# Four graph layers on one core: self loops on the adjacency's diagonal, the GCN weight behind its aggregation, two norms from one variance, and a lag of six steps

## The chip, the cores and the metric

The kernel runs on one core of a Trainium2 chip. The metric is the device time of one execution in microseconds; all times here are microseconds unless marked otherwise. The core's engines are TensorE (PE in the profile; PEld is its weight load), VectorE (DVE), ScalarE (ACT), GpSimd (POOL) and SyncE (SP). Each takes its own instructions in a fixed order, and they wait for each other by semaphores.

## What is computed

32 graphs of 512 tokens with 256 features, each with its own dense 512x512 adjacency, pass through four layers. Everything is float32. `_layernorm` has no scale or shift; `ln` is a layer norm with gamma and beta.

```
# layer 0, GIN
agg = adj @ x;   h = (1 + eps) * x + agg
x = _layernorm(x + relu(h @ W1 + b1) @ W2 + b2)          # hidden size 512
# layer 1, GCN
h = adj @ (x @ W.T + b)
x = _layernorm(x + where(h > 0, h, alpha * h))
# layer 2, GraphConv on the normalised input
h = ln(x, gamma, beta)
x = _layernorm(x + (x + relu((adj @ h) @ W_rel + b_rel + h @ W_root)))
# layer 3, GIN with RMS norm and SiLU
agg = eps * x + adj @ x
h = silu(rmsnorm(agg @ W1 + b1) * w)                     # hidden size 1024
x = _layernorm(x + h @ W2 + b2)
```

## The kernel before

The adjacency is laid out on the host so that a graph's tile `adjT` [128, 4, 512] holds, for each chunk `m` of 128 source tokens, all 512 target tokens. A token-major tile is [128, 4, 256] (four chunks of 128 tokens), a feature-major one [128, 2, 512]. PSUM has four buffers, each of two banks, for all products (`mm_feat`, `mm_tok`).

A graph is a Python generator, `graph`, that yields after each step. It has 15 steps. Layer 0 adds b2 to x on GpSimd (`xb`, L198), transposes x (L119), scales the transpose by 1+eps on ScalarE (L201), aggregates (`aggregate_feat`, L129) and sums the two on VectorE (L204); then come the hidden layer (`dense_feat`, L156, with ReLU on ScalarE, L212), the output product (`dense_tok`, L144), the residual (L216) and the norm. A norm is `row_stats` and `layernorm`: statistics for four chunks (L169, L171), variance plus epsilon (L173), the power -1/2 on GpSimd (L175), and four scaled chunks (L182). Layer 1 transposes x, multiplies by W, adds b (L227), aggregates token-major (L232), and forms the leaky ReLU with one ScalarE and two VectorE passes (L240 to L244). Layer 2 takes statistics again of the normalised x, applies gamma and beta in eight VectorE ops (L253, L256), doubles x on GpSimd (L260), transposes h, aggregates it, and multiplies both by their weights in one sum (L269). Layer 3 is like layer 0, with eight hidden chunks; each is evicted by VectorE (L295), squared by ScalarE (L300) and added up by GpSimd (L301). Products with a column of ones (L307) give the sum over features, four transposes (L319) spread 1/rms, and L323 and L324 scale and apply SiLU.

Two generators (`stream`) handle the even and the odd graphs; a loop advances them in turns, the second one step behind (`LAG = 1`). Loads of a graph are asked for two graphs ahead into three buffers. The framework's scheduler sets the order of instructions on each engine at build time, in program order as far as dependencies and free buffers allow it, and puts in the semaphores. So the loop's order matters, but the built order decides.

Of the kernel before, what the change touches and what calls it, by code (L numbers as in the profile page):

```python
# [18 lines left out]
def tile_gnn_stack(ctx: ExitStack, tc: tile.TileContext, a: dict, out: bass.AP):  # L19
    """Four adjacency layers, each with a residual and a layer norm, one graph at a time.  # L20

    Token t of a graph sits on partition t // NC in chunk t % NC, in every tile.
    Token-major tiles are [P, NC, D]; feature-major ones [P, D // P, N] with
    their columns ordered (chunk, partition).
    """
# [24 lines left out]
    def row(name):  # L50
        """A feature vector on every partition."""
        v = a[name]
        t = const.tile([P, v.shape[0]], F32, tag=name, name=name)
        nc.gpsimd.dma_start(t, v.partition_broadcast(P))
        return t

    def col(name):
        """A feature vector down the partitions, one column for each chunk of P."""
        v = a[name]
        t = const.tile([P, v.shape[0] // P], F32, tag=name, name=name)  # L60
        with nc.allow_non_contiguous_dma(reason="a small vector, once"):
            nc.gpsimd.dma_start(t, v.rearrange("(c p) -> p c", p=P))
        return t
# [11 lines left out]
    mhalf = const.tile([P, NC], F32, tag="mhalf", name="mhalf")  # L75
# [4 lines left out]
    eps3 = row("L3_gnn_epsilon")  # L80
    one_eps0 = const.tile([P, 1], F32, tag="one_eps0", name="one_eps0")
    nc.vector.tensor_scalar(one_eps0, eps0, 1.0, None, op0=ALU.add)
    nalpha = const.tile([P, 1], F32, tag="nalpha", name="nalpha")
    nc.vector.tensor_scalar(nalpha, alpha, -1.0, None, op0=ALU.mult)

    b1_0 = col("L0_gnn_b1")
    b2_0 = row("L0_gnn_b2")
    b_1 = row("L1_gnn_b")
    b_2 = row("L2_gnn_b_rel")
    g_2 = row("L2_gnn_ln_gamma")  # L90
    be_2 = row("L2_gnn_ln_beta")
    b1_3 = col("L3_gnn_b1")
    w_3 = col("L3_gnn_rms_weight")
    b2_3 = row("L3_gnn_b2")

# [7 lines left out]

    def over_tokens(t):
        return t.unsqueeze(1).to_broadcast([P, NC, D])

# [7 lines left out]
    def transposed(x):  # L114
        """Token-major x to feature-major, in PSUM."""
        ps = mm_feat()
        for j in range(DC):
            for c in range(NC):
                nc.tensor.transpose(  # L119
                    ps[:, j, c * P : (c + 1) * P], x[:, c, j * P : (j + 1) * P], ident  # L120
                )
        return ps

    def aggregate_feat(x, adjT):
        """(adj @ x) transposed, feature-major, in PSUM."""
        ps = mm_feat()
        for j in range(DC):
            for m in range(NC):
                nc.tensor.matmul(  # L129
                    ps[:, j, :],  # L130
                    x[:, m, j * P : (j + 1) * P],
                    adjT[:, m, :],
                    start=(m == 0),
                    stop=(m == NC - 1),
                )
        return ps

    def dense_tok(pairs):
        """sum of xT.T @ W over the pairs, token-major, in PSUM."""
        ps = mm_tok()  # L140
        steps = [(xT, W, k) for xT, W in pairs for k in range(W.shape[1])]
        for c in range(NC):
            for i, (xT, W, k) in enumerate(steps):
                nc.tensor.matmul(  # L144
                    ps[:, c, :],
                    xT[:, k, c * P : (c + 1) * P],
                    W[:, k, :],
                    start=(i == 0),
                    stop=(i == len(steps) - 1),
                )  # L150
        return ps

    def dense_feat(ps, i, xT, W, f):
        """Chunk f of (x @ W) transposed into slot i of a feature-major PSUM tile."""
        for k in range(DC):
            nc.tensor.matmul(  # L156
                ps[:, i, :],
                W[:, k, f * P : (f + 1) * P],
                xT[:, k, :],
                start=(k == 0),  # L160
                stop=(k == DC - 1),
            )

    def row_stats(r):
        """Mean and 1 / sqrt(variance + eps) of each token: [P, NC, 2] and [P, NC]."""
# [6 lines left out]
        ve = small.tile([P, NC], F32, tag="ve", name="ve")  # L172
        nc.vector.tensor_scalar(ve, mv[:, :, 1], LN_EPS, None, op0=ALU.add)  # L173
        rstd = small.tile([P, NC], F32, tag="rstd", name="rstd")
        nc.gpsimd.tensor_tensor(rstd, ve, mhalf, op=ALU.pow)  # L175
        return mv, rstd

    def layernorm(r, name):
        mv, rstd = row_stats(r)
        y = work.tile([P, NC, D], F32, tag=name, name=name)  # L180
        for c in range(NC):
            nc.vector.tensor_scalar(  # L182
                y[:, c, :], r[:, c, :], mv[:, c, 0:1], rstd[:, c : c + 1],
                op0=ALU.subtract, op1=ALU.mult,
            )
        return y

    def tok(name):
        return work.tile([P, NC, D], F32, tag=name, name=name)

    def feat(name):
        return work.tile([P, DC, N], F32, tag=name, name=name)

# [1 line left out]
    def graph(b, x, adjT):  # L195
        # layer 0: GIN
        xb = tok("xb")
        nc.gpsimd.tensor_add(xb, x, over_tokens(b2_0))  # L198
        pT = transposed(x)
        xT = feat("xT")  # L200
        nc.scalar.activation(xT, pT, AF.Identity, scale=one_eps0)  # L201
        pa = aggregate_feat(x, adjT)
        aT = feat("aT")
        nc.vector.tensor_add(aT, pa, xT)  # L204
        yield
        h1 = work.tile([P, FC0, N], F32, tag="h1", name="h1", bufs=1)
# [9 lines left out]
        nc.vector.tensor_add(r, ps, xb)  # L216
        x = layernorm(r, "x1")
        yield

        # layer 1: GCN  # L220
        pT = transposed(x)
        xT = feat("xT")
        nc.scalar.activation(xT, pT, AF.Copy)
        yield
        ps = dense_tok([(xT, W_1)])
        h = tok("h")
        nc.vector.tensor_add(h, ps, over_tokens(b_1))  # L227
        yield
        ps = mm_tok()
        for c in range(NC):  # L230
            for m in range(NC):
                nc.tensor.matmul(  # L232
                    ps[:, c, :],
                    adjT[:, m, c * P : (c + 1) * P],
                    h[:, m, :],
                    start=(m == 0),
                    stop=(m == NC - 1),
                )
        neg = work.tile([P, NC, D], F32, tag="neg", name="neg", bufs=1)
        nc.scalar.activation(neg, ps, AF.Relu, scale=-1.0)  # L240
        s = tok("s")
        nc.vector.scalar_tensor_tensor(s, neg, nalpha, x, op0=ALU.mult, op1=ALU.add)
        r = tok("r")
        nc.vector.scalar_tensor_tensor(r, ps, 0.0, s, op0=ALU.max, op1=ALU.add)  # L244
        x = layernorm(r, "x2")
        yield

        # layer 2: GraphConv on the normalised input
        mv, rstd = row_stats(x)
        t = tok("s")  # L250
        h = tok("h")
        for c in range(NC):
            nc.vector.scalar_tensor_tensor(  # L253
                t[:, c, :], x[:, c, :], mv[:, c, 0:1], g_2, op0=ALU.subtract, op1=ALU.mult
            )
            nc.vector.scalar_tensor_tensor(  # L256
                h[:, c, :], t[:, c, :], rstd[:, c : c + 1], be_2, op0=ALU.mult, op1=ALU.add
            )
        xx = tok("xb")
        nc.gpsimd.tensor_add(xx, x, x)  # L260
        yield
        pT = transposed(h)
        hT = feat("xT")
        nc.scalar.activation(hT, pT, AF.Copy)
        pa = aggregate_feat(h, adjT)
        aT = feat("aT")
        nc.scalar.activation(aT, pa, AF.Copy)
# [3 lines left out]
        nc.vector.tensor_add(t, ps, over_tokens(b_2))  # L271
        r = tok("r")
        nc.vector.scalar_tensor_tensor(r, t, 0.0, xx, op0=ALU.max, op1=ALU.add)
# [3 lines left out]
        # layer 3: GIN with RMS norm and SiLU  # L277
        xb = tok("xb")
        nc.gpsimd.tensor_add(xb, x, over_tokens(b2_3))
        pT = transposed(x)  # L280
        xT = feat("xT")
        nc.scalar.activation(xT, pT, AF.Identity, scale=eps3)
        pa = aggregate_feat(x, adjT)
        aT = feat("aT")
        nc.vector.tensor_add(aT, pa, xT)
# [19 lines left out]
        pq = psum.tile([P, DC, N], F32, tag="ps", name="pq")  # L305
# [8 lines left out]
        rstd = small.tile([P, NC], F32, tag="rstd", name="rstd")  # L314
        nc.gpsimd.tensor_tensor(rstd, ve, mhalf, op=ALU.pow)
        yield
        pr = psum.tile([P, DC, N], F32, tag="ps", name="pr")
# [10 lines left out]
        nc.vector.tensor_add(r, ps, xb)  # L328
# [5 lines left out]
    LAG = 1  # L334
    AHEAD = 2
    loaded = {b: load_graph(b) for b in range(min(AHEAD, B))}

# [54 lines left out]
```

## Time and profile before

| what | us |
|---|---|
| median of 3 runs (3096.54 to 3097.55) | 3096.62 |
| span of the profiled execution | 3094.4 |
| mean granted TensorE clock | 0.964 of full speed |
| L156, hidden layers: PE busy, idle before | 726.0, 51.8 |
| L144, all dense products: PE busy | 1086.9 |
| L129, feature-major aggregations: PE busy | 685.7 |
| L232, token-major aggregation: PE busy, idle before | 252.1, 28.9 |
| L119, transposes of x and of h: PE busy, idle before | 169.3, 72.4 |
| L307, sums of squares: PE busy, idle before | 43.5, 58.1 |
| L198, L260, L279, three GpSimd passes over a token tile | 75.3, 60.5, 75.4 |
| L301, GpSimd sums of squares | 284.1 (1.268 each) |
| adjacency load of a graph, issue to landing | 4.8 |

Busy time is what an engine spends inside instructions, idle is the time just before such an instruction in which the engine had nothing to do. A line number is that of the kernel above. A matmul of float32 appears as two instructions. "x8 [1.33 <-DVE x L182]" means eight instructions, before which the engine stood idle for 1.33, until VectorE finished writing x at line 182.

### The profile page before, as it was taken

To read this page: it belongs to the slowest core of one execution; us is meant where nothing else is said; L and a number is where in the kernel's file an instruction comes from. 1 tells how busy PE (TensorE), PEld (TensorE's weight loads), DVE (VectorE), ACT (ScalarE), POOL (GpSimd) and SP (SyncE) were. 2 spreads that over 40 slices of the span, in tenths; PEclk is the share of its full clock that TensorE was granted. 3 is DMA by queue.
4 is the path that set the end of the run, shared out by engine and by line. 5 is a ranking of instruction groups with operands and counts; after the bars stand their busy time and mean duration, and the time that the engine had idled before them with its cause. 6 is when DMAs were issued, how large, how long until landed. Compare 5 with 4: busy or idle time off the path is not lost.

```text
span 3094.4 us, 25923 instructions
## 1 busy us (share of the span) xinstructions
PE 2861.3 (92%) x10112; PEld 1838.1 (59%) x10112; DVE 1275.2 (41%) x3044; ACT 617.7 (20%) x834; POOL 699.3 (23%) x530
## 2 busy tenths in 40 slices
PE   8999899998999989999899999999999899998997
PEld 4556565665656656566565665647656466564654
DVE  1535335343353443434435253442534435343353
ACT  1131221212112121221212212121121211212112
POOL 1221312213031131311313113131131312313122
PEclk9999999999999999999999999999999999999998
DMA  3000000000000000000000000000000000000000
GB/s 136 28 21 8 27 28 27 28 1 27 28 28 28 8 28 21 28 28 14 28 14 27 28 14 28 14 27 28 14 28 14 28 28 14 28 7 14 14 1 14
DMA packets 17355, 73.49 MB, mean 24 GB/s; under 512 B 1937, under 2 KB 4241, under 8 KB 13137
## 3 DMA queue, kind: packets, MB, share of 16 engines
q1 hardware_dynamic: 13824, 67.12, 6.2%
q10 hardware_dynamic: 2928, 3.93, 0.4%
q8 instruction: 79, 1.29, 0.2%
q0 software_dynamic: 480, 0.80, 0.1%
q14 instruction: 44, 0.35, 0.0%
HBM read 55.06 MB, written 16.78 MB: 23 GB/s over the span
## 4 chain that ended last, share of the span: by engine, by line
PE 77%; DVE 14%; POOL 4%; ACT 3%; issue 2%; DMA 1%; POOLq 0%; ACTq 0%; DVEq 0%
PE pst L144 29%; PE psf L129 21%; PE psf L156 18%; PE pst L232 4%; PE psf L119 3%; DVE st L169 3%; DVE hT L295 2%; POOL rstd L175 2%; DVE x L182 2%; PE pq L307 1%; ACT sq L300 1%; POOL acc L301 1%; DVE h L227 1%; DVE hT L323 1%; DVE h L256 1%
## 5 line engine op out<-in xcount | busy, mean ns | idle before, releaser
L156 PE MATMUL psf<-aT,L_gnn_W 128*128 128x512 f32 x1536 | 726.0, 615 | 51.8 <-ACT sq L300 36.5
L156 PEld LDWEIGHTS psf<-aT,L_gnn_W 128*128 128x128 f32 x1536 | 283.2, 192 | 406.5 <-issue 268.0
L175 POOL TENSOR_TENSOR rstd<-ve,mhalf 128x4 f32<-128x4 f32 x160 | 165.2, 1033 | 1464.2 <-DVE ve L173 1448.1
L144 PE MATMUL pst<-L_gnn_W,hT 128*128 128x256 f32 x2048 | 480.4, 398 | 4.8 <-ACT hT L324 4.8
L129 PE MATMUL psf<-adjT,x 128*128 128x512 f32 x1024 | 458.0, 595 | 3.7 <-DMA adjT<-in_adj_dram 3.7
L144 PEld LDWEIGHTS pst<-L_gnn_W,hT 128*128 128x128 f32 x2048 | 410.3, 201 | 73.2 <-issue 7.2
L301 POOL TENSOR_TENSOR acc<-acc,sq 128x512 f32<-128x512 f32 x224 | 284.1, 1268 | 283.2 <-ACT sq L300 278.2
L129 PEld LDWEIGHTS psf<-adjT,x 128*128 128x128 f32 x1024 | 189.7, 192 | 217.0 <-issue 212.9
L295 DVE TENSOR_SCALAR hT<-psf,L_gnn_b 128x512 f32<-128x512 f32 x256 | 191.5, 748 | 251.1 <-PE psf L156 235.7
L232 PE MATMUL pst<-h,adjT 128*128 128x256 f32 x1024 | 252.1, 408 | 28.9 <-DVE h L227 28.9
L232 PEld LDWEIGHTS pst<-h,adjT 128*128 128x128 f32 x1024 | 208.3, 206 | 70.2 <-DVE h L227 39.2
L182 DVE TENSOR_SCALAR x<-r,mv,rstd 128x256 f32<-128x256 f32 x512 | 176.9, 409 | 141.7 <-POOL rstd L175 141.7
L129 PE MATMUL psf<-adjT,h 128*128 128x512 f32 x512 | 227.7, 592 | 0.0
L144 PE MATMUL pst<-L_gnn_W,h 128*128 128x256 f32 x1024 | 226.3, 379 | 0.0
L300 ACT ACTIVATE sq<-psf,L_gnn_b 128x512 f32<-128x512 f32 x224 | 146.9, 685 | 392.1 <-DVE hT L295 388.5
L328 DVE TENSOR_TENSOR r<-pst,xb 128x1024 f32<-128x1024 f32 x32 | 39.2, 1225 | 431.0 <-PE pst L144 431.0
L144 PEld LDWEIGHTS pst<-L_gnn_W,h 128*128 128x128 f32 x1024 | 193.3, 190 | 37.1 <-issue 12.3
L212 ACT ACTIVATE h<-psf,L_gnn_b 128x512 f32<-128x512 f32 x128 | 88.0, 687 | 567.5 <-PE psf L156 567.5
L198 POOL TENSOR_TENSOR xb<-x,L_gnn_b 128x1024 f32<-128x1024 f32 x32 | 75.3, 2354 | 508.4 <-DVE r L328 508.4
L324 ACT ACTIVATE hT<-hT,L_gnn_rms_weight 128x512 f32<-128x512 f32 x256 | 166.1, 713 | 78.8 <-DVE hT L323 78.7
L169 DVE BATCH_NORM_STATS2 st<-r 128x6 f32<-128x256 f32 x512 | 179.4, 413 | 2.7
L119 PE MATMUL psf<-ident,x 128*128 128x128 f32 x768 | 125.2, 282 | 48.8 <-DVE x L182 43.9
(60 smaller groups left out, 2195.4 us busy)
## 6 DMA issues: line engine op xcount, KB each, us to landing
adjT<-in_adj_dram SPq DMA_DIRECT2D x32, 1024.0 KB, 4.8
x<-in_x_dram SPq DMA_DIRECT2D x32, 512.0 KB, 3.6
out_dram<-x SPq DMA_DIRECT2D x32, 512.0 KB, 2.6
L_gnn_W<-in_L_gnn_W_dram ACTq DMA_DIRECT2D x2, 1024.0 KB, 15.7
L_gnn_W<-in_L_gnn_W_dram ACTq DMA_DIRECT2D x2, 512.0 KB, 12.2
L_gnn_b<-in_L_gnn_b_dram POOLq DMA_DIRECT2D x3, 128.0 KB, 8.0
L_gnn_W<-in_L_gnn_W_dram ACTq DMA_DIRECT2D x1, 256.0 KB, 19.9
L_gnn_W_rel<-in_L_gnn_W_rel_dram ACTq DMA_DIRECT2D x1, 256.0 KB, 20.0
```

The lines of the kernel that those rows point to most:

```text
L119: nc.tensor.transpose(ps[:, j, c * P : (c + 1) * P], x[:, c, j * P : (j + 1) * P], ident)
L129: nc.tensor.matmul(ps[:, j, :], x[:, m, j * P : (j + 1) * P], adjT[:, m, :], start=(m == 0), stop=(m == NC - 1),)
L144: nc.tensor.matmul(ps[:, c, :], xT[:, k, c * P : (c + 1) * P], W[:, k, :], start=(i == 0), stop=(i == len(steps) - 1),)
L156: nc.tensor.matmul(ps[:, i, :], W[:, k, f * P : (f + 1) * P], xT[:, k, :], start=(k == 0), stop=(k == DC - 1),)
L169: nc.vector.bn_stats(st[:, c, :], r[:, c, :])
L175: nc.gpsimd.tensor_tensor(rstd, ve, mhalf, op=ALU.pow)
L182: nc.vector.tensor_scalar(y[:, c, :], r[:, c, :], mv[:, c, 0:1], rstd[:, c : c + 1], op0=ALU.subtract, op1=ALU.mult,)
L232: nc.tensor.matmul(ps[:, c, :], adjT[:, m, c * P : (c + 1) * P], h[:, m, :], start=(m == 0), stop=(m == NC - 1),)
L295: nc.vector.tensor_scalar(hT[:, f, :], ps[:, i, :], bias, None, op0=ALU.add)
L300: nc.scalar.activation(sq, ps[:, i, :], AF.Square, bias=bias)
L301: nc.gpsimd.tensor_add(acc, acc, sq)
L324: nc.scalar.activation(hT[:, f, :], hT[:, f, :], AF.Silu, scale=w_3[:, f : f + 1])
```

## The change

Self loops: GpSimd copies the four 128x128 diagonal blocks of `adjT` into `dg` and adds a scaled identity onto the diagonal in place (`loop0`, (1+eps) times identity). So the aggregation of layer 0 gives the sum with (1+eps)x itself, and the transposes and the sum are gone. After it, the diagonal is put back from `dg`; after layer 2's aggregation, `loop3` (eps times identity) is put on it for layer 3.

GCN: `adj @ (x @ W.T + b)` becomes `(adj @ x) @ W.T + rowsum(adj) * b`. The row sums come from three GpSimd additions (`rows`) and four products with ones (`rs`).

Two norms: the input of layer 2 is the norm of a norm. Its scale follows from the first variance, so one set of statistics and one power op of eight columns give both the normalised h and the doubled x. Gamma is folded into the layer 2 weights and beta into two rows (`shift_rel`, `shift_2`) once at the start; `u` applies them with the row sums.

`aggregate` moves each half of its result out of PSUM by ScalarE as soon as that half is complete. Residual sums run in halves of the tile. `transposed` goes by chunk first. A graph has 14 steps, and the second stream starts six steps behind (`LAG = 6`). The tiles `dg`, `rows`, `u` and `v` are new; `h1` has two buffers.

```diff
+    def diagonal(adjT):
+        flat = adjT.rearrange("p m n -> p (m n)")
+        step = N + P
+        return [flat[:, m * step : m * step + P] for m in range(NC)]
...
-    mhalf = const.tile([P, NC], F32, tag="mhalf", name="mhalf")
+    mhalf = const.tile([P, 2 * NC], F32, tag="mhalf", name="mhalf")
...
+    loop0 = const.tile([P, P], F32, tag="loop0", name="loop0")
+    nc.vector.tensor_scalar(loop0, ident, one_eps0, None, op0=ALU.mult)
+    loop3 = const.tile([P, P], F32, tag="loop3", name="loop3")
+    nc.vector.tensor_scalar(loop3, ident, eps3, None, op0=ALU.mult)
...
-    g_2 = row("L2_gnn_ln_gamma")
-    be_2 = row("L2_gnn_ln_beta")
+    g_2 = col("L2_gnn_ln_gamma")
+    be_2 = col("L2_gnn_ln_beta")
...
+    def fold_norm(W, name):
+        ps = psum.tile([P, DC, N], F32, tag="ps", name="psb")
+        for k in range(DC):
+            nc.tensor.matmul(
+                ps[:, 0, 0:D],
+                be_2[:, k : k + 1].to_broadcast([P, P]),
+                W[:, k, :],
+                start=(k == 0),
+                stop=(k == DC - 1),
+            )
+        shift = const.tile([P, D], F32, tag=name, name=name)
+        nc.vector.tensor_copy(shift, ps[:, 0, 0:D])
+        for k in range(DC):
+            nc.vector.tensor_scalar(W[:, k, :], W[:, k, :], g_2[:, k : k + 1], None, op0=ALU.mult)
+        return shift
...
-        for j in range(DC):
-            for c in range(NC):
+        for c in range(NC):
+            for j in range(DC):
...
-    def aggregate_feat(x, adjT):
+    def aggregate(x, adjT):
         ps = mm_feat()
+        aT = work.tile([P, DC, N], F32, tag="aT", name="aT")
         for j in range(DC):
...
-        return ps
+            nc.scalar.activation(aT[:, j, :], ps[:, j, :], AF.Copy)
+        return aT
...
+    def inv_sqrt(ve, name):
+        n = ve.shape[1]
+        t = small.tile([P, n], F32, tag=name, name=name)
+        nc.gpsimd.tensor_tensor(t, ve, mhalf[:, 0:n], op=ALU.pow)
+        return t
+    def scaled(r, mv, s, name):
+        y = tok(name)
+        for c in range(NC):
+            nc.vector.tensor_scalar(
+                y[:, c, :], r[:, c, :], mv[:, c, 0:1], s[:, c : c + 1],
+                op0=ALU.subtract, op1=ALU.mult,
+            )
+        return y
...
+    def halves(t):
+        return [t[:, h : h + NC // 2] for h in range(0, NC, NC // 2)]
...
     def graph(b, x, adjT):
+        dg = work.tile([P, NC, P], F32, tag="dg", name="dg")
+        loops = diagonal(adjT)
+        for m in range(NC):
+            nc.gpsimd.tensor_copy(dg[:, m, :], loops[m])
+        rows = work.tile([P, N], F32, tag="rows", name="rows")
+        nc.gpsimd.tensor_add(rows, adjT[:, 0, :], adjT[:, 1, :])
+        for m in range(2, NC):
+            nc.gpsimd.tensor_add(rows, rows, adjT[:, m, :])
+        for m in range(NC):
+            nc.gpsimd.tensor_add(loops[m], dg[:, m, :], loop0)
         xb = tok("xb")
         nc.gpsimd.tensor_add(xb, x, over_tokens(b2_0))
-        pT = transposed(x)
-        xT = feat("xT")
-        nc.scalar.activation(xT, pT, AF.Identity, scale=one_eps0)
-        pa = aggregate_feat(x, adjT)
-        aT = feat("aT")
-        nc.vector.tensor_add(aT, pa, xT)
         yield
+        aT = aggregate(x, adjT)
+        for m in range(NC):
+            nc.gpsimd.tensor_copy(loops[m], dg[:, m, :])
+        yield
...
-        nc.vector.tensor_add(r, ps, xb)
+        for o, i, z in zip(halves(r), halves(ps), halves(xb)):
+            nc.vector.tensor_add(o, i, z)
         x = layernorm(r, "x1")
         yield
...
+        pq = mm_feat()
+        for c in range(NC):
+            nc.tensor.matmul(
+                pq[:, 0, c : c + 1], rows[:, c * P : (c + 1) * P], ones, start=True, stop=True
+            )
+        rs = small.tile([P, NC], F32, tag="rs", name="rs")
+        nc.vector.tensor_copy(rs, pq[:, 0, 0:NC])
+        u = tok("u")
+        for c in range(NC):
+            nc.vector.scalar_tensor_tensor(
+                u[:, c, :], shift_rel, rs[:, c : c + 1], shift_2, op0=ALU.mult, op1=ALU.add
+            )
+        aT = aggregate(x, adjT)
+        yield
+        ps = dense_tok([(aT, W_1)])
+        v = work.tile([P, NC, D], F32, tag="v", name="v", bufs=1)
+        for c in range(NC):
+            nc.vector.scalar_tensor_tensor(
+                v[:, c, :], b_1, rs[:, c : c + 1], ps[:, c, :], op0=ALU.mult, op1=ALU.add
+            )
         neg = work.tile([P, NC, D], F32, tag="neg", name="neg", bufs=1)
         s = tok("s")
         r = tok("r")
+        for o, n, i, w, z in zip(halves(r), halves(neg), halves(v), halves(s), halves(x)):
+            nc.scalar.activation(n, i, AF.Relu, scale=-1.0)
+            nc.vector.scalar_tensor_tensor(w, n, nalpha, z, op0=ALU.mult, op1=ALU.add)
+            nc.vector.scalar_tensor_tensor(o, i, 0.0, w, op0=ALU.max, op1=ALU.add)
+        mv = stats(r)
+        ve = small.tile([P, 2 * NC], F32, tag="ve2", name="ve2")
+        nc.vector.tensor_scalar(
+            ve[:, 0:NC], mv[:, :, 1], 1.0 + LN_EPS, LN_EPS * LN_EPS, op0=ALU.mult, op1=ALU.add
+        )
+        nc.vector.tensor_scalar(
+            ve[:, NC : 2 * NC], mv[:, :, 1], LN_EPS, 0.25, op0=ALU.add, op1=ALU.mult
+        )
+        q = inv_sqrt(ve, "q")
+        h = scaled(r, mv, q[:, 0:NC], "x2")
+        xx = scaled(r, mv, q[:, NC : 2 * NC], "xb")
+        yield
         pT = transposed(h)
+        hT = work.tile([P, DC, N], F32, tag="h1", name="zT")
+        for j in range(DC):
+            nc.scalar.activation(hT[:, j, :], pT[:, j, :], AF.Copy)
+        aT = aggregate(h, adjT)
+        for m in range(NC):
+            nc.gpsimd.tensor_add(loops[m], dg[:, m, :], loop3)
         yield
         ps = dense_tok([(hT, Wroot), (aT, Wrel)])
         t = tok("s")
         r = tok("r")
+        for o, i, w, z, y in zip(halves(r), halves(ps), halves(t), halves(xx), halves(u)):
+            nc.vector.tensor_add(w, i, y)
+            nc.vector.scalar_tensor_tensor(o, w, 0.0, z, op0=ALU.max, op1=ALU.add)
         x = layernorm(r, "x1")
         yield
         xb = tok("xb")
         nc.gpsimd.tensor_add(xb, x, over_tokens(b2_3))
-        pT = transposed(x)
-        xT = feat("xT")
-        nc.scalar.activation(xT, pT, AF.Identity, scale=eps3)
-        pa = aggregate_feat(x, adjT)
-        aT = feat("aT")
-        nc.vector.tensor_add(aT, pa, xT)
+        aT = aggregate(x, adjT)
         yield
...
-    LAG = 1
+    LAG = 6
     AHEAD = 2
     loaded = {b: load_graph(b) for b in range(min(AHEAD, B))}
+    shift_rel = fold_norm(Wrel, "shift_rel")
+    shift_2 = fold_norm(Wroot, "shift_2")
+    nc.vector.tensor_add(shift_2, shift_2, b_2)
```

The layer 1 lines before (L221 to L245) and the gamma and beta ops of layer 2 (L249 to L260) are taken out.

## The prediction

> **What bounds the kernel now.** The first view is the page's busy table and chain, to see which engine the time belongs to.
>
> ```profile
> span 3094.4 us, 25923 instructions
> PE 2861.3 (92%) x10112; PEld 1838.1 (59%) x10112; DVE 1275.2 (41%) x3044; ACT 617.7 (20%) x834; POOL 699.3 (23%) x530
> PE 77%; DVE 14%; POOL 4%; ACT 3%; issue 2%; DMA 1%; POOLq 0%; ACTq 0%; DVEq 0%
> ```
>
> TensorE (PE) carries the end, but the chain leaves it for a fifth of the span: those are places where PE waits for VectorE, GpSimd and ScalarE. The second view, the timeline of PE, shows where; start, length, and in brackets the idle time before and what ended it.
>
> ```profile
> 64.27 3.62 PE L144 MATMUL pst<-L_gnn_W,xT 128*128 128x256 f32 x16
> 69.21 2.19 PE L119 MATMUL psf<-ident,x 128*128 128x128 f32 x8 [1.33 <-DVE x L182]
> 79.51 3.62 PE L144 MATMUL pst<-L_gnn_W,xT 128*128 128x256 f32 x16
> 84.58 7.17 PE L232 MATMUL pst<-h,adjT 128*128 128x256 f32 x32 [1.45 <-DVE h L227]
> 109.08 1.04 PE L119 MATMUL psf<-ident,h 128*128 128x128 f32 x8
> 109.95 7.03 PE L129 MATMUL psf<-adjT,h 128*128 128x512 f32 x16
> 116.82 1.04 PE L119 MATMUL psf<-ident,x 128*128 128x128 f32 x8
> 161.25 1.05 PE L307 MATMUL pq<-ones,acc 128*128 128x1 f32 x8 [0.53 <-POOL acc L301]
> 172.52 3.60 PE L156 MATMUL psf<-aT,L_gnn_W 128*128 128x512 f32 x4 [2.42 <-ACT sq L300]
> 179.23 1.58 PE L307 MATMUL pq<-ones,acc 128*128 128x1 f32 x8 [3.10 <-POOL acc L301]
> 180.67 16.88 PE L144 MATMUL pst<-L_gnn_W,hT 128*128 128x256 f32 x64
> 205.57 13.98 PE L144 MATMUL pst<-L_gnn_W,hT 128*128 128x256 f32 x64
> 219.38 5.50 PE L156 MATMUL psf<-aT,L_gnn_W 128*128 128x512 f32 x12
> 275.77 7.17 PE L232 MATMUL pst<-h,adjT 128*128 128x256 f32 x32 [1.44 <-DVE h L227]
> ```
>
> Read prices from start to start. One f32 matmul is two instructions. A 128x512 matmul takes (116.82-109.95)/8 = 0.859; a 128x256 one (219.38-205.57)/32 = 0.432; a transpose 0.87/8 = 0.109; the four 128x1 matmuls 0.91 together. The same L232 stands at 84.58 and 275.77, so a pair of graphs lasts 191.2. A graph has 48 matmuls of 512, 88 of 256, 32 transposes, one set of 128x1 and four transposes of rstd (0.44): 41.2+38.0+3.5+0.9+0.4 = 84.1, a pair 168.2. So 23.0 of each pair is loss, and 16 pairs leave 35 for the ends. The third view splits the loss: stretches with busy PE and granted clock (the columns are length, then PE, PEld, DVE, ACT, POOL busy, then PEclk).
>
> ```profile
> 84.58:275.77 191.19, 178.24 (x632) 114.35 (x633) 79.76 (x191) 39.60 (x53) 43.26 (x32) 0.97 0.06 22
> 180.00:200.00 20.00, 20.00 (x84) 16.75 (x85) 2.57 (x6) 1.10 (x2) 2.12 (x2) 0.84 0.00 0
> ```
>
> 13.0 is plain idle. After the 2.42 and 3.10 gaps the clock is low: four L156 instructions take 3.60 where 1.72 is warm, and the 64 of L144 16.88 where 13.98 is, with 0.5 on L307: 5.3, or 2.65 a gap. The other 4 to 5 are small waits inside groups. The last view is the norm behind a dense layer, which ends at about 64.3:
>
> ```profile
> 64.47 1.23 DVE L216 TENSOR_TENSOR r<-pst,xb 128x1024 f32<-128x1024 f32 x1 [9.49 <-PE pst L144]
> 65.72 1.41 DVE L169 BATCH_NORM_STATS2 st<-r 128x6 f32<-128x256 f32 x4
> 67.05 0.36 DVE L171 BATCH_NORM_AGGREGATE mv<-st 128x2 f32<-128x6 f32 x4
> 67.44 0.17 DVE L173 TENSOR_SCALAR ve<-mv 128x4 f32<-128x4 f32 x1
> 68.74 1.38 DVE L182 TENSOR_SCALAR x<-r,mv,rstd 128x256 f32<-128x256 f32 x4 [1.12 <-POOL rstd L175]
> ```
>
> The bracket of the last line is GpSimd's power op, 1.0 long. The first chunk of x lets PE go at 69.21, 4.95 after the dense layer. The other stream's L144 covered 3.62, and PE sat 1.33: a stall is chain less cover. L232 at 84.58 had no cover at all. PE takes its instructions in a fixed order, so this subtraction can be done for the changed kernel from its built order alone.
>
> **The matmul work.** Three sets of transposes go (24x0.109 = 2.6 a graph), the layer 1 aggregation becomes 8 of 512 for 16 of 256 (6.87 for 6.91), and the row sums add a second 128x1 set (0.91). A graph has 56x0.859+72x0.432+8x0.109+1.8+0.4 = 82.3, a pair 164.7: 3.5 saved.
>
> **The other engines.** VectorE loses two aT sums and the h sum (3.7), the second statistics (2.0) and eight scalar ops at 0.48 (3.8), and gains u and v (8x0.48), xx (4x0.345) and small ones: 39.8 becomes about 36 of 100. ScalarE gains about 1.5 on 19.3. GpSimd loses xx (1.9) and gains three 128x512 adds at 1.27 and sixteen 128x128 diagonal moves, never seen; from 128x512 at 1.27 and 128x1024 at 2.35 a line gives 0.45, and the 0.20 of the one 128x128 fill at the start bounds them below; I take 0.45, the nearer in kind: 21.9 becomes 31. None becomes the bound, so these sums cost nothing as long as PE has work; where it has none, their latency is the stall. The diagonal is put back by four copies that wait for PE's last reads, and in GpSimd's queue the earlier stream's layer 2 power stands behind the first of them: it can go 4.9 after the dense product instead of 4.7, under 7.1 of cover, so nothing is lost; without that cover 0.2 is. The small loads change queue order only and stay inside the first 12.4; adj tiles take 4.8 to land and are asked for some 30 ahead.
>
> **The new stalls.** With LAG 6 of 14 steps the streams are not half a graph apart: one is 6 ahead of the other and 8 behind. In the built order of PE, for a steady pair:
>
> (a) The later stream's layer 3 aggregation stands directly behind its own layer 2 dense product. Cover 0. Chain: 4.95 plus one more pass over the tile (L273 form, 1.23) = 6.2. The halves bring nothing, since both sums stand ahead of both maxima on VectorE.
>
> (b) The earlier stream's layer 1 aggregation follows its layer 0 dense with only two 128x1 sets between, 1.8. Chain 4.95 plus the copy of rs, 0.16. Stall 3.3.
>
> (c) The later stream's layer 2 transposes follow its layer 1 dense with two transposes between, 0.22. Chain: four v ops at 0.46 (L256 takes 0.44 back to back, 0.54 for the L253 form is the other end), neg on ScalarE partly beside it, two s and two r of half size at 0.64, two of the other stream's hT products at 0.62 that the order puts among them, statistics 1.76, two ve ops 0.34, the power 1.03, first chunk 0.35, hand-overs 0.8: about 9.8. The power is now 128x8; between 1.03 and twice that, I take 1.03, because a tile this small is all fixed cost beside 128x512 at 1.27. Stall 9.6.
>
> (d) An aggregation now gives its halves to ScalarE one by one. The second half of a PSUM pair waits for the first half's eviction, as L156 does before: hand-over 0.25, activation 0.69, 0.05, so 1.0. Of eight aggregations a pair, two have no cover (1.0 each), one has four transposes (0.55), and about ten places, with those of L156, have one matmul of cover (0.2 each). The transposes of rstd add 1.2 in the later half (chain 1.6, cover 0.43). Together 5.8.
>
> Idle is 6.2+3.3+9.6+5.8 = 24.9 against 13.0. Three long gaps at 2.65 of slow clock: 8.0. In-group waits, 2 (0 to 4.4). A pair: 164.7+24.9+8.0+2 = 199.6, against 191.2.
>
> [...]
>
> **The ends.** GpSimd's queue comes free of DMA issues at 12.4; four copies, two passes, xb and a loop sum (1.8+2.5+2.35+0.45) make the first aggregation start at 19.5, where it started at 10.5. The first graph then runs alone to layer 2: 41 of matmuls, 27 of uncovered chains (4.95+8.5), evictions (5) and slow clock (3x2.65), to 87. Then 88 of matmuls of both graphs, with (c), four places of (d) and slow clock, 18, up to (a), at 193. Fifteen pairs follow, 2994. Last come (a) and the final layer 3 alone: 20.6 aggregation and W1, evictions 4.6, norm 6.0, the SiLU ramp 7.4, dense 10.4, last norm 6, store 2.6, clock 5.3: 63, with (a) 72. Sum 193+2994+72 = 3259. The profiled span is 2 under the median of the runs, so 3261.
>
> **Rivals.** *The lag covers the chains.* For it speaks that the earlier stream's layer 1 chain does get 30 matmuls of 256 (13 over 9). Against it, the order shows (a), (b), (c) bare. Without those and their clock a pair is 172.5, the time 2845. It becomes faster where the pair falls under (3094-265)/15 = 188.6, that is if 11 of the 35 lost go. Chance 0.05, and 0.02 for landing within 0.2%, which is what a measurement here can tell.
>
> *The cheap ends hold:* split evictions overlap, chains (c) 9.0 and (a) 5.6, one slow spell a pair only. A pair 192 to 194, 3145 to 3175. Chance 0.13.
>
> *GpSimd turns late.* Its power ops stand behind row sums (3.8) and xb (2.35) in its queue. In (b) the row sums end about 1.2 before the power is wanted, so twice slower diagonal moves or a late adj tile use that up. It decides once they come 1.2 later; 4 to 8 a pair, 3320 to 3380. Chance 0.15.
>
> The forecast as walked has 0.65. Its own bounds are a pair of 195.3 (no in-group waits, 1.9 of slow clock a gap, as behind the 2.42) and 203.3 (in-group 4.4, the power twice as long, v at 0.54): 3195 to 3315. The range 3165 to 3340 takes in the near part of both neighbours and leaves out the fast rival. Faster 0.05, same 0.02, slower 0.93.
>
> **What would show it.** Right: PE timeline gaps near 9.6, 6 and 3 each pair, released by DVE x2, x1, x1; PE busy lower, its idle doubled; a pair near 200; clock below 0.96. Wrong: those gaps under 3, or gaps released by POOL rows, or an aggregation waiting for adjT. If the order's groups are filled by other matmuls on the chip, the whole sum falls.

## The result and the profile after

The changed kernel takes 3334.69 us (median, 3333.78 to 3335.86) against 3096.58 for the kernel before: ratio 1.077, 95% interval 1.0755 to 1.0785, or 238 us more. The prediction was 3261 with a range of 3165 to 3340, so the time is inside, near its upper end; it lies above the forecast's own band (3195 to 3315) and in that of the rival "GpSimd turns late".

The head of the page of the changed kernel, with the engines' busy time and the shares of the chain that ended last:

```profile
span 3333.1 us, 24495 instructions
PE 2835.8 (85%) x9096; PEld 1684.2 (51%) x9096; DVE 1227.1 (37%) x3053; ACT 647.4 (19%) x1026; POOL 927.4 (28%) x1074
PE 79%; DVE 10%; POOL 5%; ACT 3%; issue 2%; DMA 1%; ACTq 0%; DVEq 0%; POOLq 0%
```

PE is busy 25.5 less than before (2861.3) in a span that is 238.7 longer, so its idle time has grown from 233 to 497. No other engine came near to being the bound. That is the form of loss that the prediction had: less matmul work, more places without any.

The timeline of PE in the changed kernel, over one steady pair of graphs; in brackets the idle time before the group and what ended it:

```profile
205.27 12.97 PE L162 MATMUL psf<-adjT,x 128*128 128x512 f32 x24 [5.91 <-DVE x L218]
...
257.54 5.41 PE L162 MATMUL psf<-adjT,x 128*128 128x512 f32 x8 [5.66 <-DVE x L218]
...
343.83 1.10 PE L162 MATMUL psf<-adjT,x 128*128 128x512 f32 x2 [1.70 <-DVE x L218]
...
349.21 3.25 PE L190 MATMUL psf<-aT,L_gnn_W 128*128 128x512 f32 x4 [1.75 <-ACT sq L352]
...
373.39 1.94 PE L151 MATMUL psf<-ident,x 128*128 128x128 f32 x8 [9.22 <-DVE x L218]
```

The three long gaps are the predicted (a), (b) and (c): 5.91 at 205, 5.66 at 257, 9.22 at 373, each released by a scaled chunk of a norm (L218 now). What the prediction did not have is the group from 343 to 349: four gaps, 3.79 in all (the two not shown are 0.17 each), ahead of and inside the later stream's layer 1 aggregation. The same (a) comes again at 409.86, so a pair takes 204.6. The view by stretches splits it (length, then busy time and instructions of PE, PEld, DVE, ACT and POOL, then granted clock and DMA):

```profile
205.27:409.86 204.59, 176.89 (x568) 104.94 (x568) 76.44 (x191) 40.30 (x64) 57.42 (x66) 0.93 0.06 21
```

Idle is 27.7. Of the busy 176.9, 164.7 is matmul work at the prices read before, and 12.2 is slow clock and waits inside groups. The clock is 0.93 over the pair, and 0.86 in the stretch from 205 to 222, behind gap (a).

Two places in the timeline of all engines of the changed kernel show why (b) and the group at 343 are longer than forecast. First (b):

```profile
251.96 1.26 POOL L244 TENSOR_TENSOR rows<-adjT 128x512 f32<-128x512 f32 x1 [3.46 <-PE psf L276]
...
253.31 1.55 DVE L283 SCALAR_TENSOR_TENSOR u<-shift_rel,rs,shift 128x256 f32<-128x256 f32 x1
253.31 2.66 POOL L246 TENSOR_TENSOR rows<-rows,adjT 128x512 f32<-128x512 f32 x2
255.93 2.15 POOL L211 TENSOR_TENSOR rstd<-ve,mhalf 128x4 f32<-128x4 f32 x2
256.98 1.38 DVE L218 TENSOR_SCALAR x<-r,mv,rstd 128x256 f32<-128x256 f32 x4 [2.13 <-POOL rstd L211]
```

The variance (L227) is ready at 253.3, but the power (L211) starts at 255.93: ahead of it in GpSimd's queue are row sums for a later graph. They in turn waited 3.46 for PE's products with ones (L276), since `rows` has two buffers and the older one is only free when those products have read it (the run with three buffers below tests this). So the row sums start just when the norm needs GpSimd. Second, the group at 343:

```profile
341.28 1.02 POOL L211 TENSOR_TENSOR rstd<-ve,mhalf 128x4 f32<-128x4 f32 x1
342.26 1.27 POOL L246 TENSOR_TENSOR rows<-rows,adjT 128x512 f32<-128x512 f32 x1
342.33 4.21 DVE L218 TENSOR_SCALAR x<-r,mv,rstd 128x256 f32<-128x256 f32 x4 [2.29 <-POOL rstd L211]
343.48 1.32 POOL L353 TENSOR_TENSOR acc<-acc,sq 128x512 f32<-128x512 f32 x1
...
344.76 1.31 POOL L246 TENSOR_TENSOR rows<-rows,adjT 128x512 f32<-128x512 f32 x1
```

The power is late here too: the variance was ready at 339.39, and the first row sum (340.06 to 341.32) stood ahead of it. Then four chunks take 4.21 where they take 1.38 in (b), 1.05 each on the mean for 0.345. One by one, three last 1.35 and one 0.40, and there are three GpSimd additions of about 1.3 beside them, two of row sums and one of the squares (L353). The 1.75 ahead of L190 follows from this: the eviction of layer 3's hidden chunk that frees PE stands behind the chunks in VectorE's queue.

### The profile page after: what moved, and what is told of

Read it like the earlier page. It is cut to its first block, busy times and chain, and to the rows that moved or that the text cites. A ratio compares the mean times of both kernels' runs of the same rounds, so it can differ in the third digit from the quotient of the medians.

```text
span 3333.1 us, 24495 instructions
## 1 busy us (share of the span) xinstructions
PE 2835.8 (85%) x9096; PEld 1684.2 (51%) x9096; DVE 1227.1 (37%) x3053; ACT 647.4 (19%) x1026; POOL 927.4 (28%) x1074
## 4 chain that ended last, share of the span: by engine, by line
PE 79%; DVE 10%; POOL 5%; ACT 3%; issue 2%; DMA 1%; ACTq 0%; DVEq 0%; POOLq 0%
PE psf L162 29%; PE pst L178 27%; PE psf L190 20%; DVE x L218 3%; ACT sq L352 2%; POOL rstd L211 2%; DVE hT L347 2%; DVE st L203 1%; PE psf L151 1%; POOL rows L244 1%; POOL rows L246 1%; ACT aT L169 1%; DVE v L291 1%; POOL q L211 1%; PE psf L276 1%
## 5 line engine op out<-in xcount | busy, mean ns | idle before, releaser
L162 PE MATMUL psf<-adjT,x 128*128 128x512 f32 x2048 | 1043.7, 655 | 251.1 <-DVE x L218 212.7
L162 PEld LDWEIGHTS psf<-adjT,x 128*128 128x128 f32 x2048 | 410.1, 210 | 793.4 <-issue 531.8
L190 PE MATMUL psf<-aT,L_gnn_W 128*128 128x512 f32 x1536 | 708.0, 605 | 37.4 <-ACT sq L352 34.1
L347 DVE TENSOR_SCALAR hT<-psf,L_gnn_b_c 128x512 f32<-128x512 f32 x256 | 191.3, 748 | 924.4 <-PE psf L190 924.3
L190 PEld LDWEIGHTS psf<-aT,L_gnn_W 128*128 128x128 f32 x1536 | 278.1, 190 | 420.3 <-issue 267.3
L353 POOL TENSOR_TENSOR acc<-acc,sq 128x512 f32<-128x512 f32 x224 | 286.2, 1278 | 660.1 <-ACT sq L352 655.0
L169 ACT ACTIVATE aT<-psf 128x512 f32<-128x512 f32 x256 | 152.8, 597 | 1469.5 <-PE psf L162 1468.6
L352 ACT ACTIVATE sq<-psf,L_gnn_b_c 128x512 f32<-128x512 f32 x224 | 146.9, 685 | 574.7 <-DVE hT L347 466.6
L218 DVE TENSOR_SCALAR x<-r,mv,rstd 128x256 f32<-128x256 f32 x384 | 176.0, 521 | 144.9 <-POOL rstd L211 144.9
L211 POOL TENSOR_TENSOR rstd<-ve,mhalf 128x4 f32<-128x4 f32 x128 | 132.1, 1036 | 224.2 <-DVE ve L227 152.1
L211 POOL TENSOR_TENSOR q<-ve,mhalf 128x8 f32<-128x8 f32 x32 | 52.4, 1638 | 493.9 <-DVE ve L308 493.9
L151 PE MATMUL psf<-ident,x 128*128 128x128 f32 x256 | 48.5, 353 | 158.2 <-DVE x L218 158.2
L374 DVE TENSOR_TENSOR hT<-hT,psf 128x512 f32<-128x512 f32 x256 | 159.3, 679 | 62.6 <-PE psf L370 62.6
L375 ACT ACTIVATE hT<-hT,L_gnn_rms_weight_c 128x512 f32<-128x512 f32 x256 | 166.8, 714 | 76.5 <-DVE hT L374 76.3
L380 DVE TENSOR_TENSOR r<-pst,xb 128x512 f32<-128x512 f32 x64 | 41.2, 686 | 355.0 <-PE pst L178 355.0
L178 PE MATMUL pst<-L_gnn_W_rel,aT 128*128 128x256 f32 x512 | 134.0, 379 | 0.0
## 6 DMA issues: line engine op xcount, KB each, us to landing
L_gnn_W_rel<-in_L_gnn_W_rel_dram ACTq DMA_DIRECT2D x1, 256.0 KB, 19.5
```

The source lines that it names most:

```text
L162: nc.tensor.matmul(ps[:, j, :], x[:, m, j * P : (j + 1) * P], adjT[:, m, :], start=(m == 0), stop=(m == NC - 1),)
L169: nc.scalar.activation(aT[:, j, :], ps[:, j, :], AF.Copy)
L178: nc.tensor.matmul(ps[:, c, :], xT[:, k, c * P : (c + 1) * P], W[:, k, :], start=(i == 0), stop=(i == len(steps) - 1),)
L190: nc.tensor.matmul(ps[:, i, :], W[:, k, f * P : (f + 1) * P], xT[:, k, :], start=(k == 0), stop=(k == DC - 1),)
L211: nc.gpsimd.tensor_tensor(t, ve, mhalf[:, 0:n], op=ALU.pow)
L218: nc.vector.tensor_scalar(y[:, c, :], r[:, c, :], mv[:, c, 0:1], s[:, c : c + 1], op0=ALU.subtract, op1=ALU.mult,)
```

## The experiments

Each ran beside the kernel before on the same chip, where that took 3098.67 to 3099.93; ratios are to it.

**LAG 1.** The whole change, with the lag of the kernel before.

```
-    LAG = 6
+    LAG = 1
```

> The changed kernel with LAG 1 in place of 6, nothing else. In its built order the norm chains have 4.4 to 7.8 of matmuls as cover instead of 0 to 1.8 in three places; chain less cover sums to 6.6 a pair where it was 19.8. Theory (the lag leaves the chains bare): a pair near 186, time 2960 to 3080, no PE gap behind a norm over 4. Rival (the cost is the new work on GpSimd and the evictions by halves, whatever the lag): 3250 or more.

3156.43 (3153.21 to 3165.99), ratio 1.019, interval 1.0172 to 1.0208: between the two. LAG 1 takes off 178 of the 238; 57 remain against the kernel before beside it. PE's timeline in this run has no gap at a layer norm over 1.63; others have come up:

```profile
915.79 3.62 PE L190 MATMUL psf<-aT,L_gnn_W 128*128 128x512 f32 x4 [3.17 <-ACT acc L349]
978.76 2.10 PE L178 MATMUL pst<-L_gnn_W,hT 128*128 128x256 f32 x4 [3.86 <-ACT hT L375]
```

In layer 3, `sq` is the squares of a hidden chunk, `acc` their sum, which starts with the first chunk's squares, and `hT` the hidden values behind SiLU; `aT` is what `aggregate` gives. Over the whole run, by the list of waits, PE waits 51.9 for ScalarE's `acc` (8.4 before), 64.0 for `hT` (4.8 before) and 34.9 for the halves of `aT`. These three add 138 and so outweigh the waits for h that are gone (51.3 before) and the 41.6 that PE's busy time is shorter. They are the subject of the runs with LAG 1 below.

**LAG 7.** One step further; the streams change roles.

```
-    LAG = 6
+    LAG = 7
```

> The changed kernel with LAG 7, exactly half of its 14 steps. Theory (what counts is the cover in the built order, and there LAG 7 has the same covers as LAG 6 with the two streams swapped: 0.0, 0.2 and 1.8): 3310 to 3360. Rival (6 of 14 was only off centre, a true half covers the chains): under 2950.

3335.23 (3334.49 to 3335.98), ratio 1.0762, interval 1.074 to 1.0784. As the order of PE says: the gaps are 5.92, 5.65 and 9.23 again.

**The kernel before, with LAG 6.**

```
-    LAG = 1
+    LAG = 6
```

> The kernel before with LAG 6 of its 15 steps, nothing else. In its built order one chain is bare: the layer 1 epilogue, norm and layer 2 norm of one stream, 13.6 long in the trace of before, has 1.4 of cover; the other norms have 6.9 or more. Theory (cover decides, each kernel has its own): idle about as before, 3050 to 3160. Rival (a lag of six costs some 240 by itself, in any kernel): 3300 or more.

3239.23 (3235.48 to 3243.9), ratio 1.0453, interval 1.0437 to 1.0469: between the two again. The lag alone costs the old kernel some 140. The gaps in its PE timeline:

```profile
948.93 1.11 PE L319 MATMUL pr<-ident,rstd 128*128 128x128 f32 x4 [7.14 <-POOL rstd L315]
953.43 0.45 PE L119 MATMUL psf<-ident,h 128*128 128x128 f32 x1 [3.38 <-DVE h L256]
```

The same double norm of layer 1 and 2 stands bare here; the other stream's transposes of 1/rms come first in PE's order and take the larger part of the wait on themselves, because the VectorE operation that prepares their power (L311, at 946.56) is queued behind the statistics of the first norm. So the theory and the rival both fail: the lag alone is neither free nor does it cost 240. Some 100 of the 238 are left for the change's parts at LAG 6.

**Three buffers for the row sums.** LAG 6 and all else as changed.

```
-        rows = work.tile([P, N], F32, tag="rows", name="rows")
+        rows = work.tile([P, N], F32, tag="rows", name="rows", bufs=3)
```

> The changed kernel with three buffers for the row sums instead of two, so that the next graph's row sums need not wait for the products with ones of the graph before last and come earlier in GpSimd's queue. Theory (in gap (b) the power op stood behind three row sums that started late for want of a buffer): the gap of 5.7 falls to 3.2, a pair loses 2 to 4, time 3270 to 3305. Rival (GpSimd is late because of the amount of its work): 3325 to 3340.

3240.05 (3239.05 to 3240.86), ratio 1.0454, interval 1.0436 to 1.0471: 95 less, or 5.9 a pair, more than the theory asked. PE's gap (b) in this run:

```profile
847.20 6.36 PE L162 MATMUL psf<-adjT,x 128*128 128x512 f32 x8 [3.37 <-DVE x L218]
```

And VectorE's four chunks at the place of the group at 343:

```profile
931.13 2.32 DVE L218 TENSOR_SCALAR x<-r,mv,rstd 128x256 f32<-128x256 f32 x4 [0.48 <-POOL rstd L211]
```

(b) is now 3.37, the 3.3 of the prediction; (c) is as it was, 9.24, (a) 5.91, and the gaps for x in the later stream's layer 1 are gone, with 0.68 of the wait for `sq` left. Over the run, PE's waits for x at L162 fall by 62.7 (212.7 to 150.0), for `sq` by 16.0, and PE's busy time by 17.6: together 96, for the 94 of the span. VectorE's busy time falls from 1227.1 to 1179.8 for the same instructions, 28.3 of it in the scaled chunks of the norms and 17.9 in `u`. The four chunks now have one GpSimd addition beside them and take 2.32; with three additions they took 4.21, with none 1.38. So each addition beside them has added 0.94 to the four, as one chunk of 1.35 for 0.40 would.

At LAG 6 the changed kernel with this buffer (3240.05) is level with the kernel before (3239.23): the 100 left for the change's parts there is the size of what the missing buffer cost.

**Late evictions in the aggregation.** LAG 6; both halves are evicted behind the matmuls of both.

```
                     stop=(m == NC - 1),
                 )
-            nc.scalar.activation(aT[:, j, :], ps[:, j, :], AF.Copy)
+        for j in range(DC):
+            nc.scalar.activation(aT[:, j, :], ps[:, j, :], AF.Copy)
```

> The changed kernel with LAG 6 as it is; only in the aggregation both evictions are issued behind the matmuls of both halves, so that the second half no longer waits for the first one's eviction. Theory (term (d) of the prediction): two places at 1.0, one at 0.55 and five at 0.2 go, 3.6 a pair or some 55, less up to 0.6 a pair where the dense layer behind waits for a later eviction: 3275 to 3305. Rival (the half-by-half eviction costs nothing, the wait is only moved behind the second half): 3325 to 3345.

3282.62 (3281.91 to 3283.52), ratio 1.0593, interval 1.0577 to 1.0609: 52 less, 3.3 a pair, where 3.6 was expected. PE's waits for `aT` at the aggregation, 38.3 over the run, are gone; those of the products behind rise only from 0.3 to 5.8. In all PE's idle time falls by 36, 2.2 a pair, and its busy time by 17 at the same mean clock (0.938). The expectation counted idle time alone, so that its sum is met is in part luck.

**LAG 1, row sums behind the layer 0 aggregation.** They are formed from the diagonal put back.

```
         dg = work.tile([P, NC, P], F32, tag="dg", name="dg")
...
-        rows = work.tile([P, N], F32, tag="rows", name="rows")
-        nc.gpsimd.tensor_add(rows, adjT[:, 0, :], adjT[:, 1, :])
-        for m in range(2, NC):
-            nc.gpsimd.tensor_add(rows, rows, adjT[:, m, :])
...
         aT = aggregate(x, adjT)
         for m in range(NC):
             nc.gpsimd.tensor_copy(loops[m], dg[:, m, :])
+        rows = work.tile([P, N], F32, tag="rows", name="rows")
+        nc.gpsimd.tensor_add(rows, adjT[:, 0, :], adjT[:, 1, :])
+        for m in range(2, NC):
+            nc.gpsimd.tensor_add(rows, rows, adjT[:, m, :])
         yield
```

> The changed kernel with LAG 1, and the row sums of the adjacency asked for behind the layer 0 aggregation instead of at the start of a graph. With LAG 1 alone (3156) the GpSimd row sums ran at 909 to 914 beside the later stream's layer 2 norm: the maximum of L330 took 2.35 for 1.29, the power came 0.74 late, and the VectorE eviction queued behind them let PE wait 3.17 and then run four matmuls at half rate. Theory (part of what is left at LAG 1 is that contention): that gap shrinks by 1.5 to 2.5 and the clock loss behind it goes in part, 1.5 to 4 a pair, so 3090 to 3132. Rival (the gap is only the length of VectorE's queue, no matter what GpSimd does): within 10 of 3156.

3122.87 (3119.25 to 3126.28), ratio 1.0077, interval 1.0062 to 1.0092: inside the theory's band at its slow end. The timeline of VectorE and GpSimd at the place, without the row sums:

```profile
903.45 2.16 POOL L244 TENSOR_TENSOR adjT<-dg,loop 128x128 f32<-128x128 f32 x4
904.62 1.54 DVE L330 SCALAR_TENSOR_TENSOR r<-s,xb 128x512 f32<-128x512 f32 x2
```

The maximum takes 1.54 for 2.35, with the four loop additions still beside it. The gap fell only from 3.17 to 2.36, less than the 1.5 to 2.5 that was expected: the other part is what the rival said, the length of VectorE's queue, in which the statistics of the norm stand ahead of the eviction. Of the 30 in the span, 15 are waits for `acc` and 15.6 PE's busy time, which fell with the clock up from 0.959 to 0.968.

**The same with late evictions** in the aggregation and in W1 of layers 0 and 3.

```
         for f0 in range(0, FC3, DC):
             ps = mm_feat()
             for i in range(DC):
                 f = f0 + i
                 dense_feat(ps, i, aT, W1_3, f)
+            for i in range(DC):
+                f = f0 + i
                 bias = b1_3[:, f : f + 1]
```

> The run with LAG 1 and later row sums, and all evictions of a PSUM pair (aggregation, W1 of layers 0 and 3) issued behind the matmuls of both halves. Theory: PE's waits for ScalarE's aT (34.9 in all with LAG 1 alone) and the small ones inside W1 groups go, 30 to 60 faster than the run without the late evictions: it would pass the kernel before, 3040 to 3095. Rival: ScalarE and VectorE then get two evictions at once, later, and what PE saved between halves it waits for behind them: within 10 of the run without, or slower.

3022.52 (3021.47 to 3023.44), ratio 0.9753, interval 0.9736 to 0.9769: 100 less than without, well past the 30 to 60. PE's idle time falls by 53.9, as expected; its busy time falls by 45.6 besides, although the mean clock did not rise (0.968 to 0.965).

**Late evictions in W1 of the kernel before**, nothing else, by the same two added lines.

> The kernel before, with the evictions of W1 of layers 0 and 3 issued behind the matmuls of both halves, nothing else. Theory: PE's waits inside these groups (0.2 and up to 2.42 at the end of layer 3) get shorter, 10 to 40 faster, 3055 to 3090. Rival: the evictions come in pairs and set the end of layer 3 anyway, within 8 of the kernel before or slower.

2992.32 (2991.72 to 2995.11), ratio 0.9658, interval 0.9644 to 0.9672: 106 less, over twice the upper end expected. A wait of the kernel before, and the busy time with the late evictions:

```profile
PE psf L156 <- ACT sq L300: 36.5, 16, 2.4
```

```profile
PE 2807.7 (94%) x10112; PEld 1843.5 (62%) x10112; DVE 1274.7 (43%) x3044; ACT 613.9 (21%) x834; POOL 700.2 (23%) x530
```

The waits for `sq` and `acc` at W1 (36.5 and 8.4 before) are gone, and those of the transposes for x fall from 43.9 to 22.8; the wait for the sum of squares grows from 58.1 to 73.0. In all PE's idle time falls by 51 and its busy time by 53.6, with the clock up from 0.964 to 0.976. If busy time goes inversely with the mean clock, an estimate, the clock makes up 35 of the 53.6. The expectation counted only the idle time, half of the gain.

**No yield at a graph's start**, added to the run with LAG 1, later row sums and late evictions.

```
         nc.gpsimd.tensor_add(xb, x, over_tokens(b2_0))
-        yield
```

> The run with LAG 1, later row sums and late evictions (3022), without the yield that the change put between the GpSimd work at a graph's start and its layer 0 aggregation; the order of PE then has that aggregation of the next graph (6.9) between the transposes of rstd and the W2 product of layer 3, as the kernel before has. Theory (what keeps LAG 1 from the kernel before with the same late evictions, 2992, is mostly that W2 stands bare behind the SiLU ramp, 3.86 a pair, 64 in all, released by ScalarE's hT): that wait goes, 2950 to 2975. Rival (GpSimd and the diagonal moves are what costs; the aggregation pulled forward waits for its loops instead): above 3000, with waits of PE for GpSimd.

2918.99 (2918.29 to 2920.0), ratio 0.9418, interval 0.9404 to 0.9432. PE's timeline without, and then with the yield:

```profile
913.92 7.03 PE L162 MATMUL psf<-adjT,x 128*128 128x512 f32 x16
920.79 1.89 PE L179 MATMUL pst<-L_gnn_W,hT 128*128 128x256 f32 x8
```

```profile
945.56 0.70 PE L179 MATMUL pst<-L_gnn_W,hT 128*128 128x256 f32 x2 [3.86 <-ACT hT L380]
```

The next graph's aggregation now stands in the time of the SiLU ramp. Over the run, waits for `hT` fall from 64.1 to 10.9, for `aT` from 11.0 to 0.7, PE's busy time by 41.2: together the span's 105. Again the busy time is the part that the expectation had too small.

**Layer 2 weights first.** The two loads stand ahead of `W1_0`.

> The same, with the two layer 2 weights loaded ahead of the others. PE stood until 23.3 for L2_gnn_W_rel (its products with beta come first in PE's order), and the first aggregation began at 26.8. Theory (the start is the product's wait in PE's queue): the first aggregation starts at 15 to 20, the whole is 7 to 12 faster than without. Rival (W1 of layer 0 now comes later and is waited for instead): within 3 of the run without.

2914.05 (2912.9 to 2915.31), ratio 0.9401, interval 0.9386 to 0.9417: 5 less. The first aggregation starts at 22.27 for 27.09, not at 15 to 20: PE's first product now waits until 18.78 for beta, a small load in GpSimd's queue.

**The change with its schedule alone altered:** LAG 1 and no yield at a graph's start, row sums and evictions as the change has them.

> The changed kernel with nothing altered but its schedule: LAG 1, and no yield between the GpSimd work at a graph's start and the layer 0 aggregation. Row sums and evictions stay as the change has them. Theory (the parts of the change pay, its order of steps costs): the run with LAG 1 alone (3156) less the W2 wait of 3.86 a pair, 53 to 64, and some 30 to 40 of slow clock behind it, as between the two runs with late evictions: 3050 to 3075, faster than the kernel before. Rival (the parts are no gain by themselves, only late evictions made them one): 3095 or more.

3095.44 (3086.72 to 3097.79), ratio 0.9983, interval 0.9973 to 0.9992. The theory falls: with its evictions by halves and its early row sums the change gains 4 over the kernel before, nothing that counts. Against the run with LAG 1 alone the wait came out as expected: `hT` falls from 64.0 to 11.5, the time by 61. The term that failed is the 30 to 40 of slow clock: PE's busy time fell by 2.0 only (2819.7 to 2817.7). The list of PE's waits in this run, with the total, the number and the longest, shows the largest that stands against the kernel before:

```profile
PE psf L190 <- ACT acc L348: 52.1, 16, 3.9
```

That is 52.1 of waits for `acc` for 8.4 before, and there are 24.6 for the split halves of `aT`. With late evictions on both sides and the row sums moved, the change is ahead: 2919 against 2992, by 73.

## Why the prediction came out as it did

**Less matmul work.** Right: 164.7 a pair at the old prices fits the order, and PE's busy time fell (2861.3 to 2835.8) although its mean clock was lower (0.938 for 0.964).

**(a), 6.2.** Right: 5.91, and the same with three `rows` buffers. **(c), 9.6.** Right: 9.22, but in part by luck: the power of eight columns takes 1.64, not the 1.03 of "all fixed cost", and the rest of the chain came out 1.0 shorter than the sum.

**(b), 3.3.** This is the step that failed. It measured 5.66. The prediction said that "the row sums end about 1.2 before the power is wanted". It named only slower diagonal moves or a late adjacency tile as what could hold them up. What they waited for is the release of the `rows` buffer by the products with ones, which comes late. With a third buffer (b) is 3.37. The rival "GpSimd turns late" named the queue and the price, 4 to 8 a pair and 3320 to 3380, which is where the time fell, and had another cause for it.

**The gaps at 343, 3.8 a pair.** Not forecast. The prediction wrote that the other engines' sums "cost nothing as long as PE has work", and took each VectorE operation at the price it has alone. Here the power came 1.9 late behind a row sum, and a chunk with a GpSimd addition beside it takes 1.35 for 0.40. The third buffer took away the gaps for x and most of that for `sq`; with what (b) lost and the busy time, that is the 5.9 a pair.

A `u` operation shows the same: the one at 253.31 lasts 1.55 beside two row sums, the one at 346.65, with no addition beside it, 0.48. Why these operations take longer beside an addition on GpSimd no run here shows.

**(d), 5.8.** Too large: by PE's timeline over the pair, 0.25, 0.75 and 0.90 in front of aggregations, 0.17 at W1 and 0.81 at the transposes of 1/rms, some 2.9. Tried alone, the aggregations' share is 2.2 of idle time and 1.1 of busy time a pair.

**Clock and waits in groups, 10.0.** 12.2 measured; (b) is longer and there is a fourth place, but no run here splits it. The 2.65 a gap was read somewhat high, as it sets the length 3.60 of four instructions against 1.72 from start to start; as lengths it is 3.60 against 1.98. The pair: a -0.3, b +2.4, c -0.4, d -2.9, the new gaps +3.8, clock and the rest +2.4: 5.0 more than 199.6. The mean of the fifteen pairs is 204.3, so 70 in all.

**The ends.** The start took 199.4 for 193, as the first aggregation began at 25.5 and not at 19.5: the products of `fold_norm` stand ahead of it in PE's order and waited until 21.98 for a weight. The first step was read from GpSimd's queue alone. The end behind the last (a) took 63 as walked, and with (a) 69 for 72. Start +6, pairs +70 and end -3 are the 74 between 3259 and the span.

**The range.** That the time lies inside it is in part luck: the oversized (d), 2.9 a pair or some 44, stood against what (b) and the group at 343 added, and the upper end of 3340 had been set with that rival in mind.

**The lag covers the chains.** Rightly given 0.05: LAG 1 does but for gaps of up to 1.63, LAG 6 and 7 do not. The lag is the larger part of the loss, and alone costs the old kernel 140. The shares overlap: LAG 1 takes off 178, yet at LAG 6 the third buffer alone takes off 95.

What stays open: how the 57 that LAG 1 leaves divide among the change's single parts. They were tried by place (row sums, evictions, first yield), not one by one against the kernel before.

## What to carry to other kernels

In a kernel whose engines run fixed orders, a stall can be read off the built order as chain less cover; but follow each wait in that order to the buffer that it is for, since a small tile with one buffer too few can put work of another graph into the queue just ahead of what everybody needs. When two streams are shifted, look for the matmuls that stood in the way of each norm and count whether they still do. And before splitting an eviction for latency, see whether the next matmuls into the other half then wait for it: here issuing both evictions behind both halves gained 106 in the old kernel, more than the 73 by which the change is ahead of it after that. 2914 is the fastest version run.

## What the hardware showed unasked

Where PE's idle time fell, its busy time fell too, but at no fixed price:

| step | idle | busy | mean clock |
|---|---|---|---|
| kernel before, late evictions in W1 | -51 | -54 | 0.964 to 0.976 |
| LAG 1, row sums later | -15 | -16 | 0.959 to 0.968 |
| late evictions added to that | -54 | -46 | 0.968 to 0.965 |
| first yield taken out of that | -64 | -41 | 0.965 to 0.977 |
| LAG 6, three buffers for the row sums | -76 | -18 | 0.938 to 0.944 |
| LAG 1, first yield taken out | -62 | -2 | 0.959 to 0.960 |

So a price per gap, such as the 2.65 of the prediction, does not carry from one schedule to the next. The length of a single gap doesn't decide it either. The four instructions behind the gap of 3.17 at LAG 1 took 3.62; four of the same kind at 921.82 of that run, with no gap before them, took 1.88. Two later gaps of the same length, the first from that run and the second from the run with LAG 1 and no first yield, differ:

```profile
951.04 1.98 PE L190 MATMUL psf<-aT,L_gnn_W 128*128 128x512 f32 x4 [2.28 <-ACT sq L352]
```

```profile
936.25 3.64 PE L190 MATMUL psf<-aT,L_gnn_W 128*128 128x512 f32 x4 [2.27 <-ACT sq L351]
```

What decides it these runs do not show.
